# Layer 1's q and k made with the tokens stationary and 512 weight columns moving, turned through DRAM, in a two-layer graph attention kernel

## The chip, the core and the metric

The kernel runs on one core of one Trainium2 chip. The core has five engines with instruction queues of their own, each worked off in order: TensorE (PE) multiplies matrices, VectorE (DVE) and ScalarE (ACT) work element by element and may read PSUM, where PE leaves its results, GpSimd (POOL) works element by element on SBUF, and SyncE (SP) issues the transfers (DMAs) between DRAM and SBUF. They wait for each other by semaphores. The metric is the device time of one execution in microseconds (us), as the median of several runs.

## What is computed

Two layers of masked attention, each followed by a residual sum and a normalisation over the 512 features. x is 128 graphs of 128 nodes and 512 features, adj a mask of 128 by 128 for each graph; all numbers are 32-bit floats.

```python
# layer 0: 4 heads of 64
q, k, v = x @ Wq, x @ Wk, x @ Wv
sim = where(adj, q @ k.T * 64**-0.5, -max)
x = layernorm(x + softmax(sim) @ v @ Wo + bo)
# layer 1: 8 heads of 64
h = layernorm(x) * gamma + beta
q, k, v = split(h @ w_qkv.T)
s = where(adj | eye, q @ k.T * 64**-0.5, -1e9)
x = layernorm(x + softmax(s) @ v @ w_out.T + b_out)
```

## The kernel before

Graphs are handled in groups of two (G = 2, so 256 tokens and 64 groups). Every group goes through a pipeline of steps; step(s) (line 736) is the body for s = 2 to 63, opening (line 698) is what stands before it, closing (line 825) runs twice and last (line 879) once. A step works on several groups at once: layer 0's projections (product_0) of group s, layer 0's scores and softmax of group s-1, its attention and output projection (out_product(0, ...)) of group s-2, layer 1's q and k (qk) of group s-2, layer 1's scores, softmax and v of group s-3, its attention and output projection (out_product(1, ...)) of group s-4.

All projections are written as seven half-size products instead of eight (Strassen's scheme in Winograd's form): sums of halves of the left operand are made on POOL (halves_sums, line 286), those of the weights once at the start. The seven products, numbered 1 to 7 and issued in the order 1, 2, 6, 5, 7, 3, 4, share three PSUM banks: "a", "f" and one of four turning "mm" tiles ("c", INTO in line 297). A product that adds to a bank must wait until the reader of the bank's earlier state is done. ACT copies the banks after products 1, 5 and 6, DVE adds after 2, 3 and 7, ACT copies after 4 (taken, line 333; for layer 0 in lines 392 to 399). Layer 1's q and k come out of PE with features on the partitions: 128 weight columns are stationary and 128 tokens move, eight matmuls a product, each of them two passes on PE (32-bit floats). For v the 128 tokens are stationary and 256 weight columns move.

A transpose of activations or probabilities goes through DRAM: DVE turns 32 by 32 blocks (turn in line 214, blocks in line 523), put (line 201) writes the tile to DRAM, and fetch (line 207) brings it back in four transfers of 32 partitions each, blocks now in place. arrive (line 223) does this for the rows of either layer into the one tile "raw"; probs_arrive for the probabilities. in_order (line 240) and finish (line 249) are ACT's copies out of raw: into xT of layer 0, and with gamma and beta into xT of layer 1. For the first and the last two groups finish_direct (line 264) transposes on PE instead.

The order in which the functions are called is written out by hand, and each engine gets its instructions in that order; nothing is reordered. All transfers are issued by SP, in order: a transfer whose source or target isn't ready holds up those behind it. So where a call stands in step matters on every engine that it uses. Tiles with one tag and one buffer (pool one) are shared by their users in turn. The residual rows of a group stay in R (a ring of six buffers, line 78); load brings the next group's rows and mask, stats (line 601) makes mean and variance on DVE and then, by roots, the reciprocal root on POOL, norms (line 639) normalises on ACT, deferred to the next flush, addend (line 589) scales (layer 1, ACT) and adds the bias (POOL).

Of the kernel before, what the change touches and what calls it, by code (L numbers as in the profile page):

```python
# [17 lines left out]
P = 128  # L18
D = 64
G = 2  # L20
# [7 lines left out]
def kernel(ctx: ExitStack, tc: tile.TileContext, x, adj, wq, wk, wv, wo, bo,  # L28
# [13 lines left out]
    six = ctx.enter_context(tc.tile_pool(name="six", bufs=6))  # L42
    dram = ctx.enter_context(tc.tile_pool(name="dram", bufs=2, space=bass.MemoryType.DRAM))
# [26 lines left out]
    for i in range(4):  # L70
        spare_rows(six, "r", 2)
    for tag, n in (("qk1", 4), ("v1", 2), ("xT1", 2)):
        spare_rows(one, tag, n)

    def load(g):
        if g >= NG:
            return
        R[g] = six.tile([P, G, E], F32, tag="r", name=f"r_{g}")
        M[g] = six.tile([P, G, N], U8, tag="m", name=f"m_{g}")
        nc.sync.dma_start(R[g], x[g * G:(g + 1) * G].rearrange("b n e -> n b e"))  # L80
        nc.sync.dma_start(M[g], adj[g * G:(g + 1) * G].rearrange("b i j -> i b j"))

    R[0] = six.tile([P, G, E], F32, tag="r", name="r_0")
# [30 lines left out]
    gb_raw = const.tile([2 * KC, P], F32, name="gb_raw")  # L114
# [3 lines left out]
    def load_transposed(dst, src, name, scaled=0):  # L118
# [7 lines left out]
        def part(r):  # L126
# [6 lines left out]
            if r * P < scaled:  # L133
                nc.scalar.activation(to, pt, AF.Copy, scale=SCALE)
            elif r % 2:
                nc.scalar.copy(to, pt)
            else:
                nc.vector.tensor_copy(to, pt)
# [17 lines left out]
    w1qk = w1[:, :, :2 * I1].rearrange("p c (t h f) -> p c t h f", t=2, h=2)  # L156
    w1v = w1[:, :, 2 * I1:].rearrange("p c (h f) -> p c h f", h=2)
    wsqk = const.tile([P, 3, KH, 2, I1 // 2], F32, name="wsqk")
    wsv = const.tile([P, 3, KH, I1 // 2], F32, name="wsv")

    def weight_sums(w, ws, *blocks_):

        for c in blocks_:
            if w is w1qk:
                b11, b12 = w[:, c, :, 0], w[:, c, :, 1]
                b21, b22 = w[:, KH + c, :, 0], w[:, KH + c, :, 1]
            else:
                b11, b12 = w[:, c, 0], w[:, c, 1]
                b21, b22 = w[:, KH + c, 0], w[:, KH + c, 1]
# [20 lines left out]
    load_transposed(w1, w_qkv, "w_qkv", scaled=INNER[1])  # L190
# [6 lines left out]
    RATIO, XT, QK, V, QKV = {}, {}, {}, {}, {}  # L197
# [102 lines left out]
    def product(kind, g, i):  # L300
# [6 lines left out]
        w, ws = (w1qk, wsqk) if kind == "qk" else (w1v, wsv)  # L307

        def right(c):
            return {1: lambda: w[:, c, :, 0] if kind == "qk" else w[:, c, 0],  # L310
                    2: lambda: w[:, KH + c, :, 0] if kind == "qk" else w[:, KH + c, 0],
                    3: lambda: w[:, KH + c, :, 1] if kind == "qk" else w[:, KH + c, 1],
                    4: lambda: ws[:, 2, c], 5: lambda: w[:, c, :, 1] if kind == "qk" else w[:, c, 1],
# [8 lines left out]
        if kind == "qk":  # L322
            todo = [(acc[:, (t * 2 + j) * P:(t * 2 + j + 1) * P], right(c)[:, t, j * P:(j + 1) * P],
                     left[:, c], c) for t in range(2) for j in range(2) for c in range(KH)]
        else:
            todo = [(acc[:, :I1 // 2], left[:, c], right(c), c) for c in range(KH)]
        for n, (o, lhsT, rhs, c) in enumerate(todo):

            nc.tensor.matmul(o, lhsT, rhs, start=first and n == 0, stop=n == len(todo) - 1,  # L329
                             skip_group_check=True)  # L330
        taken(kind, g, i, acc)

    def taken(kind, g, i, acc):

        if i == 1:
            if kind == "qk":
                QK[1, g] = one.tile([P, 2 * I1 // P, T], F32, tag="qk1", name=f"qk1_{g}")
            else:
                V[1, g] = one.tile([P, G, I1], F32, tag="v1", name=f"v1_{g}")
        n = 512 if kind == "qk" else I1 // 2  # L340
        src = acc[:, :n]

        def whole(b, h):
            if kind == "qk":

                return QK[1, g].rearrange("p (t h j) n -> p t h j n", t=2, h=2)[:, :, h, :, b * N:(b + 1) * N]
            return V[1, g][:, b, h * n:(h + 1) * n]

        def like(ap, b, h):
            return ap.rearrange("p (t j n) -> p t j n", t=2, j=2) if kind == "qk" else ap  # L350

        if i in (1, 5, 6):
            e = one.tile([P, 512], F32, tag=f"e{i}", name=f"e{kind}{i}_{g}")[:, :n]
            EV[kind, i] = e
            nc.scalar.copy(e, src)  # L355
        elif i == 4:
            nc.scalar.copy(whole(1, 0), like(src, 1, 0))
        elif i in (2, 3, 7):
            b, h, e = {2: (0, 0, 1), 3: (0, 1, 6), 7: (1, 1, 5)}[i]
            nc.vector.tensor_add(whole(b, h), like(src, b, h), like(EV[kind, e], b, h))  # L360

    def product_0(g, *which):
# [5 lines left out]
        for i in which:  # L368
# [5 lines left out]
            if i == 1:  # L374

                QKV[g] = two.tile([P, G, 2, 3, P], F32, tag="qkv0", name=f"qkv0_{g}")
# [4 lines left out]
            acc = ACC[0, bank]  # L381
            todo = [(t, c) for t in range(3) for c in range(KH)]
            for n, (t, c) in enumerate(todo):
                lhsT, rhs = (right[:, c, t], left[:, c]) if t < 2 else (left[:, c], right[:, c, t])
                nc.tensor.matmul(acc[:, t * P:(t + 1) * P], lhsT, rhs, start=first and n == 0,  # L385
# [3 lines left out]
            def whole(b, h):  # L389
                return QKV[g][:, b, h].rearrange("p t n -> p (t n)")  # L390
# [44 lines left out]
    def group_of(s, part):  # L435
        g = s - (3 if part else 1)
# [517 lines left out]
```

## Time and profile before

| what | value |
|---|---|
| median of 3 runs | 2784.76 us (2784.01 to 2785.39) |
| the profiled execution: span from first to last instruction | 2782.9 us (the execution's own time; the median stands 1.9 us above it) |
| PE, DVE, ACT, POOL busy | 99%, 64%, 54%, 63% |
| a step, from first score matmul to the next step's | 42.84 us |
| DMA | 405 MB, mean 146 GB/s, packets take 49.5% of 16 engines' span in the kernel's queue |
| a transfer of 512 KB to DRAM, a fetch of 128 KB: issue to landing | 3.0 to 4.4 us, 3.6 to 4.1 us (medians) |

The page gives busy time of each engine, the chain of work that ended last, and groups of like instructions with their mean duration. A timeline line has start (us), duration (us), engine, line of the kernel, operation, output and inputs, shapes and count; in brackets stands the idle time before it and what ended it. Matmuls overlap on PE, so what a product costs is read from one start to the next, not from the durations. In a table by stretches, each line has the stretch, the busy time of each engine with its count of instructions, the granted clock of PE, and last the DMA share and the rate in GB/s.

### The profile page before, as it was taken

The page shows a single profiled execution, that of the slowest core. Times are in us where ns is not written, and L with a number is a line of the kernel's source. Part 1 is how long each engine was busy: PE and PEld are TensorE (multiplying, and loading weights), DVE is VectorE, ACT ScalarE, POOL GpSimd, SP SyncE. Part 2 cuts the span into 40 slices and gives each one's busy share as a digit, 9 for nine tenths or more (in the row PEclk, how much of TensorE's full clock was granted, in tenths as well). Part 3 has the DMA queues.
Part 4 walks back from the last instruction along what each step waited for, and adds up shares of the span by engine and source line. Part 5 has one row for each costly group of instructions (what it writes and reads, how often), then busy time and mean ns, then how long its engine had stood idle before and what let it go on. Part 6 is the DMA issues. An engine that isn't in the chain of part 4 may idle for free.

```text
span 2782.9 us, 63227 instructions
## 1 busy us (share of the span) xinstructions
PE 2768.0 (99%) x23317; PEld 2609.2 (94%) x23317; DVE 1789.9 (64%) x3303; ACT 1502.5 (54%) x4811; POOL 1752.2 (63%) x2311
## 2 busy tenths in 40 slices
PE   9999999999999999999999999999999999999998
PEld 8999999999999999999999999999999999999997
DVE  5766666666666666666666666666666666666665
ACT  3554555645555556455555564555555645555554
POOL 5656566666565666666656666666566666665664
PEclk9999999999999999999999999999999999999999
DMA  5345455464564554644545546455454464554532
GB/s 170 115 138 173 128 158 154 130 175 138 138 171 127 161 153 129 177 138 138 169 129 161 153 127 177 139 138 166 128 165 148 128 179 136 145 165 126 160 107 69
DMA packets 281812, 405.24 MB, mean 146 GB/s; under 512 B 44696, under 2 KB 206496, under 8 KB 281504
## 3 DMA queue, kind: packets, MB, share of 16 engines
q1 hardware_dynamic: 281504, 401.20, 49.5%
q8 instruction: 185, 3.03, 0.5%
q14 instruction: 123, 1.01, 0.1%
HBM read 205.00 MB, written 196.08 MB: 144 GB/s over the span
## 4 chain that ended last, share of the span: by engine, by line
PE 96%; issue 1%; POOL 1%; DVE 1%; DMA 1%; ACT 0%; SPq 0%; POOLq 0%; ACTq 0%; DVEq 0%
PE qka L329 16%; PE a L385 12%; PE oa L423 12%; PE qkf L329 8%; PE va L329 8%; PE av L575 6%; PE f L385 6%; PE of L423 6%; PE qkc L329 4%; PE vf L329 4%; PE c L385 3%; PE oc L423 3%; PE sc L456 2%; PE sc L462 2%; PE vc L329 2%; PE sc_a L462 2%
## 5 line engine op out<-in xcount | busy, mean ns | idle before, releaser
L514 POOL TENSOR_TENSOR sm<-sm,rec 128x1024 f32<-128x1024 f32 x192 | 364.1, 1896 | 383.4 <-DVE rec L513 383.1
L505 ACT ACTIVATE sm<-sm,nmax 128x128 f32<-128x128 f32 x1536 | 595.2, 393 | 4.9 <-DVE nmax L496 4.3
L596 POOL TENSOR_TENSOR r<-r,bias 128x1024 f32<-128x1024 f32 x128 | 302.0, 2359 | 63.5 <-ACT r L595 63.5
L427 DVE TENSOR_TENSOR r<-oa,r 128x256 f32<-128x256 f32 x508 | 212.3, 418 | 199.7 <-PE oa L423 191.6
L292 POOL TENSOR_TENSOR xs<-xT 128x256 f32<-128x256 f32 x256 | 189.4, 740 | 211.0 <-ACT xT L246 164.9
L505 ACT ACTIVATION_READ_ACCUMULATOR sm<-sm,nmax 128x1 f32 x1536 | 294.8, 192 | 0.0
L355 ACT COPY eqk<-qka 128x512 f32<-128x512 f32 x128 | 75.0, 586 | 349.3 <-PE qka L329 349.3
L490 DVE COPY_PREDICATED sm<-m,sc 128x512 f32<-128x512 uint8 x256 | 173.0, 729 | 134.9 <-PE sc L456 134.9
L329 PE MATMUL qka<-xs,wsqk 128*128 128x128 f32 x2048 | 249.7, 275 | 0.3 <-POOL xs L292 0.3
L329 PE MATMUL qkf<-xs,w 128*128 128x128 f32 x2048 | 249.8, 275 | 0.0
L529 DVE STREAM_TRANSPOSE turnedp<-sm 128x1024 f32<-128x1024 f32 x189 | 234.0, 1238 | 17.1 <-DMA scrp<-turnedp 11.8
L329 PEld LDWEIGHTS qka<-xs,wsqk 128*128 128x128 f32 x2048 | 239.0, 192 | 0.5 <-POOL xs L292 0.5
L329 PEld LDWEIGHTS qkf<-xs,w 128*128 128x128 f32 x2048 | 239.0, 192 | 0.0
L360 DVE TENSOR_TENSOR qk<-qka,eqk 128x512 f32<-128x512 f32 x64 | 44.3, 692 | 291.1 <-PE qka L329 286.1
L496 DVE TENSOR_REDUCE nmax<-sm 128x8 f32<-128x1024 f32 x192 | 226.4, 1206 | 0.1
L423 PE MATMUL oa<-wso,so 128*128 128x256 f32 x760 | 206.0, 380 | 0.7 <-DVE r L427 0.7
L423 PE MATMUL of<-wo,so 128*128 128x256 f32 x760 | 205.6, 379 | 0.7 <-POOL so L292 0.7
L615 POOL TENSOR_SCALAR ve<-mv 128x2 f32<-128x2 f32 x191 | 40.8, 214 | 261.3 <-DVE mv L608 255.1
L641 ACT ACTIVATE r<-r,shift,root 128x512 f32<-128x512 f32 x254 | 192.4, 807 | 8.7 <-POOL shift L630 4.7
L476 POOL MEMSET sm<- 128x1024 f32 x192 | 178.8, 951 | 0.0
L607 DVE BATCH_NORM_STATS2 st<-r 128x6 f32<-128x512 f32 x254 | 171.7, 676 | 4.4
L423 PEld LDWEIGHTS of<-wo,so 128*128 128x128 f32 x760 | 144.1, 190 | 20.9 <-POOL so L292 1.1
(159 smaller groups left out, 6799.9 us busy)
## 6 DMA issues: line engine op xcount, KB each, us to landing
scrp<-turnedp SPq DMA_DIRECT2D x189, 512.0 KB, 3.0
pT<-scrp SPq DMA_DIRECT2D x756, 128.0 KB, 4.1
scr<-turned SPq DMA_DIRECT2D x121, 512.0 KB, 4.4
raw<-scr SPq DMA_DIRECT2D x484, 128.0 KB, 3.6
r<-in_x_dram SPq DMA_DIRECT2D x63, 512.0 KB, 3.9
out_dram<-r SPq DMA_DIRECT2D x63, 512.0 KB, 5.0
m<-in_adj_dram SPq DMA_DIRECT2D x64, 32.0 KB, 3.7
raw_r<-in_L_gnn_w_qkv_dram SPq DMA_DIRECT2D x8, 256.0 KB, 4.2
```

What stands on the lines that cost most here:

```text
L292: nc.gpsimd.tensor_tensor(o, a0, a1, op=op)
L329: nc.tensor.matmul(o, lhsT, rhs, start=first and n == 0, stop=n == len(todo) - 1, skip_group_check=True)
L385: nc.tensor.matmul(acc[:, t * P:(t + 1) * P], lhsT, rhs, start=first and n == 0, stop=n == len(todo) - 1, skip_group_check=True)
L423: nc.tensor.matmul(acc, left[:, c], right[:, c], start=first and c == 0, stop=c == hk - 1, skip_group_check=True)
L427: nc.vector.tensor_add(part, acc, part)
L476: nc.gpsimd.memset(sm, NEG1 if part else NEG0)
L496: nc.vector.tensor_reduce(NMAX[part], SM[part], AX.X, ALU.max, negate=True)
L505: nc.scalar.activation(sm[:, i, k, :], sm[:, i, k, :], AF.Exp, bias=nmax[:, i, k:k + 1], accum_out=total[:, i, k:k + 1])
L514: nc.gpsimd.tensor_tensor(SM[part], SM[part], rec[:, :, :, None].to_broadcast([P, 2, K1, N]), op=ALU.mult)
L529: nc.vector.transpose(t.rearrange("p q (h r) -> p q h r", r=32), SM.pop(part).rearrange("p i k (q r) -> p q (i k) r", r=32))
L596: nc.gpsimd.tensor_tensor(R[g], R[g], (bias0, bias1)[l][:, None, :].to_broadcast([P, G, E]), op=ALU.add)
L641: nc.scalar.activation(R[g][:, b], R[g][:, b], AF.Identity, bias=shift[:, b:b + 1], scale=root[:, b:b + 1])
```

## The change

Layer 1's q and k are now made as v is: 128 tokens are stationary and 512 weight columns move, so a product has two matmuls in place of eight. The half split of the weight columns is now k (first) and q (second). The results have tokens on the partitions, so they are turned: DVE transposes 32 by 32 blocks after products 2, 7, 3 and 4 (taken_tokens), SP puts k of each graph and q of both to DRAM, q_arrive and k_arrive fetch them, and ACT copies q in order with the scale (q_in_order); k is used from the fetched tile as it lies. The scale 64**-0.5 is no longer in the weights. The last two groups (PLAIN_QK) keep the old form. Layer 1 works on a group one step later: qk on s-3 with v on s-3, scores on s-4, attention and output on s-5; there are three closing steps, and layer 1's rows always go through DRAM. Calls in step stand in a new order: norms of layer 1, load and both halves of finish now stand among layer 0's products, qk stands where v stood, and v with layer 1's output projection stands at the end of the step, with layer 1's stats and addend behind them.

To make room, layer 0's q, k and v have one buffer (qkv0) in which v alternates between two places, several tiles share tags (so and aT of layer 0 with the two tiles of q, the turned q with raw, the turned k with xT0), R gets a seventh buffer and layer 1's v a second one. closing has the same changes of order as step; it isn't shown.

```diff
+    seven = ctx.enter_context(tc.tile_pool(name="seven", bufs=7))
     dram = ctx.enter_context(tc.tile_pool(name="dram", bufs=2, space=bass.MemoryType.DRAM))
     ps_mm = ctx.enter_context(tc.tile_pool(name="ps_mm", bufs=4, space=PSUM))
...
-        spare_rows(six, "r", 2)
-    for tag, n in (("qk1", 4), ("v1", 2), ("xT1", 2)):
-        spare_rows(one, tag, n)
+        spare_rows(seven, "r", 2)
+    for pool, tag, n in ((one, "kt", 2), (two, "v1", 2), (two, "v1", 2), (one, "xT1", 2)):
+        spare_rows(pool, tag, n)
...
@@ -153,20 +152,17 @@
     I1 = INNER[1]
     KH = KC // 2
 
-    w1qk = w1[:, :, :2 * I1].rearrange("p c (t h f) -> p c t h f", t=2, h=2)
+    w1qk = w1[:, :, :2 * I1].rearrange("p c (h f) -> p c h f", h=2)
...
@@ -319,45 +315,111 @@
         elif first:
             ACC[kind, which] = ps_st.tile([P, 512], F32, tag=which, name=f"{kind}{which}_{g}")
         acc = ACC[kind, which]
-        if kind == "qk":
-            todo = [(acc[:, (t * 2 + j) * P:(t * 2 + j + 1) * P], right(c)[:, t, j * P:(j + 1) * P],
-                     left[:, c], c) for t in range(2) for j in range(2) for c in range(KH)]
+        n = I1 if kind == "qk" else I1 // 2
+        if kind == "qk" and g in PLAIN_QK:
+            todo = [(acc[:, j * P:(j + 1) * P], right(c)[:, j * P:(j + 1) * P], left[:, c])
+                    for j in range(K1) for c in range(KH)]
         else:
-            todo = [(acc[:, :I1 // 2], left[:, c], right(c), c) for c in range(KH)]
-        for n, (o, lhsT, rhs, c) in enumerate(todo):
-
-            nc.tensor.matmul(o, lhsT, rhs, start=first and n == 0, stop=n == len(todo) - 1,
+            todo = [(acc[:, :n], left[:, c], right(c)) for c in range(KH)]
+        for m, (o, lhsT, rhs) in enumerate(todo):
+            nc.tensor.matmul(o, lhsT, rhs, start=first and m == 0, stop=m == len(todo) - 1,
                              skip_group_check=True)
-        taken(kind, g, i, acc)
-
-    def taken(kind, g, i, acc):
+        (taken_v if kind == "v" else taken_features if g in PLAIN_QK else taken_tokens)(g, i, acc[:, :n])
+
+    PLAIN_QK = (NG - 2, NG - 1)
+
+    def tap(kind, g, i, src, scale=1.0):
+        EV[kind, i] = one.tile([P, 512], F32, tag=f"e{i}", name=f"e{kind}{i}_{g}")[:, :src.shape[1]]
+        if scale == 1.0:
+            nc.scalar.copy(EV[kind, i], src)
+        else:
+            nc.scalar.activation(EV[kind, i], src, AF.Copy, scale=scale)
+
+    def taken_v(g, i, src):
 
         if i == 1:
-            if kind == "qk":
-                QK[1, g] = one.tile([P, 2 * I1 // P, T], F32, tag="qk1", name=f"qk1_{g}")
-            else:
...
+        if i == 4:
+            nc.scalar.copy(to, src)
+        else:
+            nc.vector.tensor_add(to, src, EV["v", e])
+
+    QO, KT, TQ, SCRQ = {}, {}, {}, {}
+
+    def taken_tokens(g, i, src):
+
+        if i in (1, 5, 6):
+            return tap("qk", g, i, src)
+        if i == 4:
+            done = src
+        else:
+            done = EV["qk", {2: 1, 3: 6, 7: 5}[i]]
+            nc.vector.tensor_add(done, src, done)
+        what, b = {2: ("k", 0), 7: ("q", 1), 3: ("q", 0), 4: ("k", 1)}[i]
+        if i in (2, 7):
+            TQ[what] = one.tile([P, 4, G, K1 * 32], F32, tag={"k": "xT0", "q": "raw"}[what],
+                                name=f"t{what}_{g}")
+            SCRQ[what] = dram.tile([P, 4, G, K1 * 32], F32, tag=f"scr{what}", name=f"scr{what}_{g}")
+        t = TQ[what][:, :, b]
+        nc.vector.transpose(t.rearrange("p q (c j) -> p q c j", j=32),
+                            done.rearrange("p (c q j) -> p q c j", q=4, j=32))
+        if what == "k":
+            nc.sync.dma_start(SCRQ[what][:, :, b], t)
+        elif i == 3:
+            nc.sync.dma_start(SCRQ[what], TQ[what])
+
+    def k_tile(g):
+        KT[g] = one.tile([P, 4, G, K1, 32], F32, tag="kt", name=f"kt_{g}")
+        return KT[g]
+
+    def q_tile(g, b):
+        QO[g, b] = one.tile([P, K1, N], F32, tag=f"qo{b}", name=f"qo{b}_{g}")
+        return QO[g, b]
+
+    def q_arrive(g):
+
+        if 0 <= g < NG and g not in PLAIN_QK:
+            RAW["q"] = one.tile([P, 4, G, K1, 32], F32, tag="raw", name=f"rawq_{g}")
+            fetch(RAW["q"].rearrange("p a b c j -> p a (b c j)"), SCRQ["q"].rearrange("p q b x -> p q (b x)"))
+
+    def k_arrive(g):
+
+        if 0 <= g < NG and g not in PLAIN_QK:
+            fetch(k_tile(g).rearrange("p a b c j -> p a (b c j)"), SCRQ["k"].rearrange("p q b x -> p q (b x)"))
+
+    def q_in_order(g):
+
+        if 0 <= g < NG and g not in PLAIN_QK:
+            for b in range(G):
+                nc.scalar.activation(q_tile(g, b).rearrange("p c (a j) -> p a c j", a=4), RAW["q"][:, :, b],
+                                     AF.Copy, scale=SCALE)
+
...
+    def taken_features(g, i, src):
+
+        if i in (1, 5, 6):
...
-            nc.scalar.copy(whole(1, 0), like(src, 1, 0))
-        elif i in (2, 3, 7):
-            b, h, e = {2: (0, 0, 1), 3: (0, 1, 6), 7: (1, 1, 5)}[i]
-            nc.vector.tensor_add(whole(b, h), like(src, b, h), like(EV[kind, e], b, h))
+            nc.scalar.copy(plain_keys(g, 1), src)
+        else:
+            b, e = {3: (0, 6), 7: (1, 5)}[i]
+            nc.vector.scalar_tensor_tensor(q_tile(g, b).rearrange("p c n -> p (c n)"), src, SCALE,
+                                           EV["qk", e], op0=ALU.mult, op1=ALU.add)
 
     def product_0(g, *which):
+            odd = g % 2
             todo = [(t, c) for t in range(3) for c in range(KH)]
             for n, (t, c) in enumerate(todo):
                 lhsT, rhs = (right[:, c, t], left[:, c]) if t < 2 else (left[:, c], right[:, c, t])
-                nc.tensor.matmul(acc[:, t * P:(t + 1) * P], lhsT, rhs, start=first and n == 0,
+                at = (t + odd) % 3
+                nc.tensor.matmul(acc[:, at * P:(at + 1) * P], lhsT, rhs, start=first and n == 0,
                                  stop=n == len(todo) - 1, skip_group_check=True)
             src = acc[:, :3 * P]
 
             def whole(b, h):
-                return QKV[g][:, b, h].rearrange("p t n -> p (t n)")
+                return qkv0[:, b, h, 1 - odd:4 - odd].rearrange("p t n -> p (t n)")
...
     def group_of(s, part):
-        g = s - (3 if part else 1)
+        g = s - (4 if part else 1)
...
-                        q_, k_ = (QKV[g][r, b, h // 2, i, :] for i in range(2))
+                        q_, k_ = (qkv0[r, b, h // 2, i, :] for i in (1, 2))
                         nc.tensor.matmul(ps[h % 2][:, b * K0 + h // 2, :], q_, k_, start=True, stop=True)
             else:
-                t = slice((part - 1) * N, part * N)
+                b = part - 1
                 for h in range(HEADS[1]):
                     r = slice((h % 2) * D, (h % 2 + 1) * D)
-                    q_, k_ = (QK[1, g][r, i * K1 + h // 2, t] for i in range(2))
-                    nc.tensor.matmul(ps[h % 2][:, h // 2, :], q_, k_, start=True, stop=True)
+                    nc.tensor.matmul(ps[h % 2][:, h // 2, :].rearrange("p (a j) -> p a j", j=32),
+                                     QO[g, b][r, h // 2], keys_of(g, b, h // 2, r), start=True, stop=True)
...
-            g = s - (2, 4)[l]
+            g = s - (2, 5)[l]
             if not 0 <= g < NG:
                 continue
             K = (K0, K1)[l]
             if part != 2:
-                AT[l, g] = one.tile([P, G, K, N], F32, tag=f"aT{l}", name=f"aT{l}_{g}")
+                AT[l, g] = one.tile([P, G, K, N], F32, tag=("qo1", "aT1")[l], name=f"aT{l}_{g}")
...
-        so = SO[l, g] = one.tile([P, 4, K // 2, N], F32, tag=("so", "xs0")[l], name=f"so{l}_{g}")
+        so = SO[l, g] = one.tile([P, 4, K // 2, N], F32, tag=("qo0", "xs0")[l], name=f"so{l}_{g}")
...
     def step(s):
 
-        direct = s in (2, 3)
         made = scores(s)
-        load(s + 1)
         if s > 2:
             in_order(s)
             sums(0, s)
+        arrive(1, s - 3)
         masked(made, s, 0, 1, 2)
         attend(s)
-        maxima(s, 0)
-        if s > 3:
-            maxima(s, 1)
+        maxima(s, 0, 1)
         out_sums(0, s - 2)
         exps(s, 0, 0)
         product_0(s, 1)
         exps(s, 0, 1)
         out_product(0, s - 2, 1, 2, 5)
-        if s == 3:
-            maxima(s, 1)
         maxima(s, 2)
         product_0(s, 2)
+        flush()
+        load(s + 1)
         normalised(s, 0)
         out_product(0, s - 2, 6, 3)
         exps(s, 1, 0)
         stats(0, s - 2, 0)
         product_0(s, 6)
         exps(s, 1, 1)
+        finish(s - 3, 0)
         out_product(0, s - 2, 7)
         product_0(s, 5)
         out_product(0, s - 2, 4)
         stats(0, s - 2, 1)
         exps(s, 2, 0)
         product_0(s, 7)
-        exps(s, 2, 1)
+        finish(s - 3, 1)
         normalised(s, 1)
         product_0(s, 3)
         blocks(s, 0)
-        flush()
+        exps(s, 2, 1)
         product_0(s, 4)
-        if direct:
+        if s in (2, 3):
             prepare(len(setup) - (s == 2))
-        else:
-            turn(1, s - 2)
-        out_sums(1, s - 4)
-        v(s - 3, 1, 2)
-        out_product(1, s - 4, 1)
-        if not direct:
-            arrive(1, s - 2)
         blocks(s, 1)
-        probs_arrive(s, 0)
-        v(s - 3, 6, 5)
-        out_product(1, s - 4, 2)
-        normalised(s, 2)
-        v(s - 3, 7, 3)
-        turn(0, s + 1)
-        v(s - 3, 4)
-        flush(latest)
-        cleared(s + 1, 0, 1)
-        if direct:
-            finish_direct(s - 2)
-        else:
-            finish(s - 2, 0)
+        qk(s - 3, 1)
         if s == 2:
             weight_sums(w1qk, wsqk, 1)
             prepare(1)
-        out_product(1, s - 4, 6, 5)
-        if not direct:
-            finish(s - 2, 1)
-        out_product(1, s - 4, 7, 3, 4)
+        flush()
+        qk(s - 3, 2)
+        normalised(s, 2)
+        probs_arrive(s, 0)
+        qk(s - 3, 6, 5)
+        flush(latest)
+        turn(1, s - 2)
+        probs_arrive(s, 1)
+        qk(s - 3, 7)
+        cleared(s + 1, 0, 1)
+        out_sums(1, s - 5)
         blocks(s, 2)
-        probs_arrive(s, 1)
-        stats(1, s - 4, 0)
-        stats(1, s - 4, 1)
+        qk(s - 3, 3, 4)
+        out_product(1, s - 5, 1, 2)
+        q_arrive(s - 3)
+        v(s - 3, 1, 2)
+        out_product(1, s - 5, 6)
+        turn(0, s + 1)
+        k_arrive(s - 3)
+        probs_arrive(s, 2)
+        v(s - 3, 6, 5)
+        out_product(1, s - 5, 5)
+        v(s - 3, 7, 3)
+        q_in_order(s - 3)
+        out_product(1, s - 5, 7)
+        v(s - 3, 4)
         arrive(0, s + 1)
-        probs_arrive(s, 2)
         cleared(s + 1, 2)
+        out_product(1, s - 5, 3, 4)
         addend(0, s - 1)
+        stats(1, s - 5, 0)
+        stats(1, s - 5, 1)
+        addend(1, s - 4)
         with_self(s - 2)
-        qk(s - 2, 1, 2, 6)
-        flush()
-        qk(s - 2, 5)
-        addend(1, s - 3)
-        qk(s - 2, 7, 3, 4)
...
+    for s in range(NG, NG + 3):
+        closing(s)
```

## The prediction

> **What bounds the kernel now.** I read the head of the page first, then the chain that ended last, then one step of the timeline, then SP's waits and the DMA issues.
>
> ```profile
> span 2782.9 us, 63227 instructions
> PE 2768.0 (99%) x23317; PEld 2609.2 (94%) x23317; DVE 1789.9 (64%) x3303; ACT 1502.5 (54%) x4811; POOL 1752.2 (63%) x2311
> ...
> PE 96%; issue 1%; POOL 1%; DVE 1%; DMA 1%; ACT 0%; SPq 0%; POOLq 0%; ACTq 0%; DVEq 0%
> ```
>
> TensorE (PE) is busy 99% of the span and is 96% of the last chain; the waits of PE name nine causes, 8.0 us in all. So any step in which another engine makes PE wait is lost time at once. The span stands 1.9 us under the median of the runs (2784.76); I work in differences and put them on the median. The timeline of one step:
>
> ```profile
> 1435.24 1.16 PE L456 MATMUL sc<-qkv 64*128 64x128 f32 x16
> 1437.05 0.73 POOL L292 TENSOR_TENSOR xs<-xT 128x256 f32<-128x256 f32 x1 [2.66 <-ACT xT L246]
> ...
> 1440.05 0.46 POOL L292 TENSOR_TENSOR so<-aT 128x128 f32<-128x128 f32 x1
> ...
> 1440.89 1.16 PE L385 MATMUL a<-xT,w 128*128 128x128 f32 x8
> ...
> 1443.20 0.59 PE L423 MATMUL of<-wo,so 128*128 128x256 f32 x2
> ...
> 1453.40 1.03 PE L329 MATMUL va<-w,xT 128*128 128x256 f32 x4
> 1454.26 1.03 PE L329 MATMUL vc<-w,xT 128*128 128x256 f32 x4
> ...
> 1465.49 1.95 PE L329 MATMUL qka<-xT,w 128*128 128x128 f32 x16
> ...
> 1467.27 1.95 PE L329 MATMUL qkc<-xT,w 128*128 128x128 f32 x16
> ...
> 1468.94 0.27 POOL L615 TENSOR_SCALAR ve<-mv 128x2 f32<-128x2 f32 x1 [1.31 <-DVE mv L608]
> ...
> 1470.52 0.95 POOL L476 MEMSET sm<- 128x1024 f32 x1
> 1471.44 2.37 POOL L596 TENSOR_TENSOR r<-r,bias 128x1024 f32<-128x1024 f32 x1
> ...
> 1478.08 1.16 PE L456 MATMUL sc<-qkv 64*128 64x128 f32 x16
> ```
>
> First column start, second duration. A step takes 42.84 us (1435.24 to 1478.08), start to start. A qk product (16 PE passes of 128 columns) takes 1.785 from start to start, 111.6 ns a pass; a v product (4 passes of 256) takes 0.863, 215.8 ns a pass. GpSimd (POOL) starts the four sums of xT (3.0 us) only 1.8 us into the step, then the sums of aT; the first of these is ready at 5.35, and the product that needs it (of<-wo,so) starts at 7.96. These 2.6 us are the slack I shall spend. SP and the DMAs:
>
> ```profile
> SPq L210 <- DMA scr<-turned: 162.2, 61, 4.4
> ```
>
> ```profile
> scrp<-turnedp SPq DMA_DIRECT2D x189, 512.0 KB, 3.0
> pT<-scrp SPq DMA_DIRECT2D x756, 128.0 KB, 4.1
> scr<-turned SPq DMA_DIRECT2D x121, 512.0 KB, 4.4
> raw<-scr SPq DMA_DIRECT2D x484, 128.0 KB, 3.6
> ```
>
> ```profile
> 1473.00:1475.00 2.00, 2.00 (x21) 2.00 (x20) 0.31 (x1) 1.80 (x4) 0.93 (x2) 1.00 1.15 215
> ```
>
> A fetch waits on SP for its put to land, 2.7 us a time, and all that SP issues later stands behind. The last line is a 2 us stretch late in the step: its last two numbers are the DMA share, 1.15, and 215 GB/s: the DMA engines are full there already.
>
> **The change part by part.** E is the moment at which a step's first score matmul starts.
>
> *Products.* Seven qk products a group become 4 passes of 512 columns each, for 62 groups (the last two keep the old form). No row has 512. The straight line through 111.6 and 215.8 gives 424 ns, so 1.70 a product; twice the 256-column pass gives 1.726. I take 1.712: 0.073 saved, 0.51 a step (0.41 to 0.62), 32 us in 62 groups. The Trainium skill ("TensorE: Matmul & The Clock Gate", Back-to-back issue gap) gives sustained figures of 81 ns at 128 columns and 131 ns at 512, by which the qk passes would shrink to 0.40 of today's 12.5 us, a saving of 7.5 a step; the step from 111.6 to 215.8 here denies such a discount.
>
> *ACT.* One copy of 0.59 goes, two in-order copies of q (about 0.6 each, row xT<-raw) come. Moved ahead of the evictions of layer 0: the norms of layer 1 (1.41) and the two halves of finish (1.04 each). From the first exp to the end of the copy of product_0(5), in the new order: 16 exps of 0.385 (6.2), two copies (0.7), norms (1.4), half of finish (1.0) and the copy itself (0.4): 9.7 us, where today it is 7.2. product_0(3) writes the same bank and waits for it; below.
>
> *DVE.* Four transposes of 128x512 a group, 0.67 each (row L219's), 2.7 us a step on an engine busy 64%. They cost PE nothing where DVE runs ahead; the next user of bank "a" (v's product 1) comes 1.73 us of PE after qk(4), and the last transpose ends about 1.2 after it: 0.5 of cover, and past this each us is a us. The statistics of layer 1 (two of 0.79) and with_self (0.35) now stand after the step's last product, so masking starts at E+2.6, not E+1.25.
>
> *POOL, the first chain.* Today layer 1's statistics precede qk and 12 us of PE cover what hangs on them. Now out_product(1,...,4) is the last product. From E: DVE add 0.25+0.4, statistics 1.6, so roots may start at E+2.3; roots 1.6 (1468.94 to 1470.52), addend(1) 2.37, sums(0) 3.0, first out_sum 0.54, semaphore 0.1: E+9.9. The product that needs it is due at E+7.97 (row above). PE waits 1.9 us in every step. This is already more than the 0.51 saved.
>
> *SP and DMA, the second chain.* Three puts and eight fetches come to a step, 2 MB on 6.3 MB. The one tile raw holds layer 1's rows, then q turned, q fetched, and only then the next group's rows, in a row. Let T be the end of qk(4), 12.1 us (14 products of 0.863) before E. q's transpose is done at T+0.55 (DVE is late by blocks(1), whose POOL product stands behind sums(1)); its put lands 4.4 later by the row, or up to 6 later, since two fetch sets of 512 KB (2.3 us each at 224 GB/s) and two puts (1.3 each) are issued in the 4.7 us ahead of it; I take T+6.5. Behind it on SP: q's fetch 1.76, a put 0.4, k's fetch 1.76, pT's 2.0, then the next rows' fetch, last issue 1.3 later, landing 3.6: T+17.4, E+5.3; 6.1 with the queue still full, 3.7 if the put takes the row's 4.4. ACT in_order takes 1.2, then sums(0), out_sum: E+8.6 to E+11.05 for the same product. So PE's wait is 1.9 to 3.1; I take 2.9, near the upper end, since the stretch was full before the change. ACT's first exp comes at E+8.7 then (in_order, three copies), product_0(3) may start at E+18.5 and is due at 15.5+2.9: no more is lost there. k's fetch lands about E+1.9 with its scores due at E+1.0; that wait lies inside the 2.9. [...]
>
> *Bought with nothing.* The load of x after a wait for out (4.6 us on SP, moved to about E+14 to E+19): the next put is due at E+21; without that cover up to 4 us. One buffer for layer 0's q, k, v: read before E+4, written after E+8. Seventh R buffer, weight layout: no added work.
>
> *Ends.* Four groups of direct transposes go: 32 of 0.11, 3.6 us. Step 2 has no qk, so step 3 meets its probabilities and rows early: 13 us of waits; steps 4 and 5 have the q round trip with only 6 us of v as cover: about 14. A third closing step has 22.3 us of PE and a softmax chain of near 28; with the two before it about 19. In all 46, between 20 and 60.
>
> *Sum.* 2784.8 - 32 - 3.6 + 58 steps x 2.9 (168) + 46 = 2963.
>
> **The rivals.** *Both chains hidden.* POOL reaches the sums in time, or ACT and DMA run ahead. For it: POOL is busy only 63%, and no engine but PE is full. Against: the first chain has no DMA in it and every link has a row. It decides where PE's wait falls below 0.5 a step: then 2784.8 - 35.6 + 20 = 2769, on the other side (2750 to 2795).
>
> *Only the first chain.* Rows arrive in time: 58 x 1.9, ends 35: 2894. This lies in my forecast's own range.
>
> *DMA full for good.* 2 MB more at 215 GB/s are 9.7 us in a tail of 20: if the rows come at E+8, the wait is 5 and the time 3085. Against: DMA is busy under half of the span.
>
> *512 columns don't stream.* If a pass takes 446 ns or more the 32 us are gone; 512-column rows are missing, so this can't be excluded, and it lifts every case by 32.
>
> **How the numbers follow.** Slower by the chains (2865 to 3035): 0.78. Both hidden: 0.15, of which 0.12 faster, 0.02 same, 0.01 slower. DMA full: 0.07. A difference under 0.2% (5.6 us) can't be told from none. The range leaves out the hidden case and the worst: 2860 to 3035. Chances: faster 0.12, same 0.02, slower 0.86.
>
> **What would show it.** Steps 45.2 apart; PE's share near 93%; PE waiting for POOL's so and for ACT's xT at the head of each step (about 1 to 3 us a step together), for kt at the scores; SP waiting for the put of q; the qk pass near 429 ns. A step of 42.4 with no such waits would make me wrong, and a step of 44.2 would say that only POOL's chain binds.

## The result, and the profile after

The changed kernel takes 3121.77 us (median of 4 runs, 3109.18 to 3122.88), the kernel before 2784.43: a ratio of 1.12, 95% interval 1.1181 to 1.122. The forecast was slower, 2963 us with a range of 2860 to 3035. The direction holds, the size doesn't: the loss is 337 us where 178 were forecast.

The profiled execution spans 3107.4 us. It was the fastest of the four (3109.18 us): the median lies 12.6 us above it, and what sets the executions 14 us apart isn't known. Head of the page, busy time and the last chain:

```profile
span 3107.4 us, 54173 instructions
PE 2864.2 (92%) x18077; PEld 2233.8 (72%) x18077; DVE 1944.9 (63%) x3545; ACT 1525.3 (49%) x4871; POOL 1744.5 (56%) x2311
...
PE 51%; DMA 20%; ACT 7%; POOL 7%; DVE 6%; SPq 6%; issue 4%; ACTq 0%; DVEq 0%; POOLq 0%
```

PE fell from 96% to 51% of the chain that ended last, and DMA came in with 20%. No compute engine has a higher share than before (only the packets of the DMA queue do, 58.4% for 49.5%): this is a kernel of waits. Where the 324.5 us between the spans (3107.4 - 2782.9) lie is read from the first score matmul of each step: 6.2 up to step 6, 281.7 in the 58 steps 6 to 63 (4.86 each: 47.71 for 42.85), 36.6 from step 64 to the end. One step on PE, from the timeline:

```profile
1393.38 1.16 PE L517 MATMUL sc<-qkv 64*128 64x128 f32 x16
1396.38 0.46 PE L522 MATMUL sc_a<-kt,qo 64*128 64x128 f32 x2 [1.83 <-DMA kt<-scrk]
1397.56 0.34 PE L522 MATMUL sc_f<-kt,qo 64*128 64x128 f32 x1 [0.72 <-DMA kt<-scrk]
...
1398.53 2.06 PE L522 MATMUL sc<-kt,qo 64*128 64x128 f32 x15
...
1403.88 1.16 PE L446 MATMUL a<-xT,w 128*128 128x128 f32 x8
...
1406.22 0.70 PE L484 MATMUL of<-wo,so 128*128 128x256 f32 x2
...
1417.08 1.88 PE L325 MATMUL qka<-w,xT 128*128 128x512 f32 x4
1418.80 1.88 PE L325 MATMUL qkc<-w,xT 128*128 128x512 f32 x4
...
1441.28 0.94 PE L517 MATMUL sc<-qkv 64*128 64x128 f32 x12
```

With E = 1393.38, PE waits for k's fetch at the scores of layer 1, then the second graph's scores and the attention go slowly, and the product that needs the sums of aT (of<-wo,so) starts at E+12.84, where it was E+7.96. So 4.88 us are gone by then. The same head of the step on POOL and ACT:

```profile
1395.61 0.27 POOL L676 TENSOR_SCALAR ve<-mv 128x2 f32<-128x2 f32 x1 [7.60 <-DVE mv L669]
...
1397.22 2.36 POOL L657 TENSOR_TENSOR r<-r,bias 128x1024 f32<-128x1024 f32 x1
...
1401.51 1.14 ACT L243 COPY xT<-raw 128x512 f32<-128x512 f32 x2 [6.60 <-DMA raw<-scr]
...
1402.72 0.73 POOL L289 TENSOR_TENSOR xs<-xT 128x256 f32<-128x256 f32 x1 [3.15 <-ACT xT L243]
...
1405.71 0.46 POOL L289 TENSOR_TENSOR so<-aT 128x128 f32<-128x128 f32 x1
```

Roots start at E+2.2 and addend ends at E+6.2, but then POOL stands idle for 3.15 us: the rows of the group land only at E+8.1. In this step the first sum of aT ends just when PE has come to the product, so it looks as if the late rows and the late k held PE to the same moment. They do so only in some steps. Three steps later PE is at the product early and waits:

```profile
1536.74 1.16 PE L517 MATMUL sc<-qkv 64*128 64x128 f32 x16
...
1546.33 1.16 PE L446 MATMUL a<-xT,w 128*128 128x128 f32 x8 [1.26 <-ACT xT L243]
...
1550.36 0.70 PE L484 MATMUL of<-wo,so 128*128 128x256 f32 x2 [1.56 <-POOL so L289]
```

Over steps 6 to 63 the product starts 0.51 us behind the start of the first sum of aT in 56 of 58 steps, so it is the rows that hold PE; k comes last only in the other two. Late in the step shown first, DVE finishes q's second transpose and SP goes on:

```profile
1427.64 2.69 SPq L207 DMA_DIRECT2D pT<-scrp  x4
...
1429.11 0.71 DVE L368 STREAM_TRANSPOSE tq<-eqk 128x512 f32<-128x512 f32 x1
...
1430.43 0.45 SPq L201 DMA_DIRECT2D scrp<-turnedp  x1
1430.98 0.38 SPq L373 DMA_DIRECT2D scrq<-tq  x1
1431.45 0.85 SPq L371 DMA_DIRECT2D scrk<-tk  x1
1436.21 2.87 SPq L207 DMA_DIRECT2D rawq<-scrq  x4
1439.18 0.38 SPq L201 DMA_DIRECT2D scr<-turned  x1
1439.66 2.21 SPq L207 DMA_DIRECT2D kt<-scrk  x4
1441.97 1.80 SPq L207 DMA_DIRECT2D pT<-scrp  x4
1443.88 1.81 SPq L207 DMA_DIRECT2D raw<-scr  x4
```

SP puts q and the second half of k, stands for 3.9 us until q has landed, and then issues q's fetch, k's and the rows' one behind the other. That q's four fetches take 2.87 us to issue is not typical: the median over the steps is 1.75.

### The profile page after: what moved, and what is told of

It reads as the page before. It is cut to its first block, busy times and chain, and to the rows that moved or that the text cites. A ratio compares the mean times of both kernels' runs of the same rounds, so it can differ in the third digit from the quotient of the medians.

```text
span 3107.4 us, 54173 instructions
## 1 busy us (share of the span) xinstructions
PE 2864.2 (92%) x18077; PEld 2233.8 (72%) x18077; DVE 1944.9 (63%) x3545; ACT 1525.3 (49%) x4871; POOL 1744.5 (56%) x2311
## 3 DMA queue, kind: packets, MB, share of 16 engines
q1 hardware_dynamic: 430208, 535.46, 58.4%
## 4 chain that ended last, share of the span: by engine, by line
PE 51%; DMA 20%; ACT 7%; POOL 7%; DVE 6%; SPq 6%; issue 4%; ACTq 0%; DVEq 0%; POOLq 0%
PE qka L325 11%; DMA kt<-scrk 7%; PE a L446 7%; DMA raw<-scr 6%; SPq L207 5%; POOL xs L289 5%; PE qkf L325 5%; PE f L446 5%; DMA scrq<-tq 5%; PE oa L484 4%; ACT sm L566 3%; PE qkc L325 3%; PE va L325 3%; PE of L484 3%; PE c L446 2%
## 5 line engine op out<-in xcount | busy, mean ns | idle before, releaser
L334 ACT COPY ev<-va 128x256 f32<-128x256 f32 x128 | 47.6, 372 | 581.2 <-PE va L325 581.2
L243 ACT COPY xT<-raw 128x512 f32<-128x512 f32 x122 | 69.4, 616 | 364.3 <-DMA raw<-scr 299.3
L488 DVE TENSOR_TENSOR r<-of,r 128x256 f32<-128x256 f32 x254 | 107.7, 424 | 206.5 <-PE of L484 199.4
L325 PE MATMUL qkf<-w,xs 128*128 128x512 f32 x496 | 233.1, 592 | 0.0
L325 PE MATMUL qka<-wsqk,xs 128*128 128x512 f32 x496 | 233.1, 592 | 0.0
L398 ACT ACTIVATE qo<-rawq 128x512 f32<-128x512 f32 x124 | 71.2, 621 | 321.8 <-DMA rawq<-scrq 321.8
L325 PEld LDWEIGHTS qkf<-w,xs 128*128 128x128 f32 x496 | 94.3, 190 | 118.6 <-issue 118.3
L325 PEld LDWEIGHTS qka<-wsqk,xs 128*128 128x128 f32 x496 | 94.3, 190 | 118.1 <-issue 103.5
```

Of the source, the lines that this page charges most:

```text
L325: nc.tensor.matmul(o, lhsT, rhs, start=first and m == 0, stop=m == len(todo) - 1, skip_group_check=True)
L488: nc.vector.tensor_add(part, acc, part)
```

## The experiments

e1 to e6, e8 and e9 are one execution each, beside the kernel before on the same chip; e7 and e10 are timed in rounds. Step times are means from step 5 on. Executions of the changed kernel lie 14 us apart, 0.2 us a step, so smaller differences between single executions say little.

**e1_plain and e2_noturn: the order of calls, and the form.** e1 needs one line:

```diff
-    PLAIN_QK = (NG - 2, NG - 1)
+    PLAIN_QK = tuple(range(NG))
```

> The changed kernel with every group in the old form of q and k (128 weight columns stationary, straight into feature order), so no transposes, puts, fetches or in-order copies of q and k; the new order of calls and the turn's delay stay. My theory: the step of 47.7 us is set by the loop q's put, q's fetch, k's fetch, scores (and beside it the next rows behind q in the one tile raw). With the loop gone POOL's chain is left, 1.9 us a step: step 44.7, about 2915 us (2880 to 2940). Rival, the order of calls itself (POOL and ACT behind the step's last product) makes the loss: still 3050 or more. Rival, the 512-column passes make the loss: step 42.8, about 2800.

e2 keeps the 512-column products and their additions and cuts what follows:

```diff
         if i == 4:
-            done = src
+            nc.vector.tensor_copy(FIX["e"], src)
         else:
             done = EV["qk", {2: 1, 3: 6, 7: 5}[i]]
             nc.vector.tensor_add(done, src, done)
-        what, b = {2: ("k", 0), 7: ("q", 1), 3: ("q", 0), 4: ("k", 1)}[i]
...
-                    nc.tensor.matmul(..., QO[g, b][r, h // 2], keys_of(g, b, h // 2, r), ...)
+                    nc.tensor.matmul(..., FIX["k"]..., FIX["k"][r, :, b, h // 2], ...)
```

> The changed kernel with the 512-column products of q and k and their additions, but without their transposes, puts, fetches and in-order copies: the scores of layer 1 read one constant tile instead, so the output is not the reference's. It differs from e1_plain by the form of the products and little else. My theory: 7 products of 1.717 for 7 of 1.785, so 0.48 us a step under e1_plain, about 2885 (POOL's chain stays). Rival, 512 columns cost more than their passes show: no faster than e1_plain.

Measured: 2935.88 and 2907.25 us, steps of 44.92 and 44.44. PE's longest wait in e1, then in e2:

```profile
PE of L484 <- POOL so L289: 97.4, 62, 3.1
```

```profile
PE of L461 <- POOL so L289: 98.3, 62, 3.1
```

Once in each of the 62 steps, 1.6 us, PE waits for the sums of aT: the new order of calls, with the turn's delay and the tiles that go with it, costs 2.07 us a step. The form gives 0.48 a step, 28.6 us in all, as forecast. e1 lies 21 us over my figure, more than half of it since the step is 44.92 and not 44.7 (58 x 0.22 are 13), the rest at the ends.

**e3_stale: the wait apart from the traffic.**

```diff
-                TQ[what] = one.tile(..., tag={"k": "xT0", "q": "raw"}[what], ...)
+                TQ[what] = one.tile(..., tag={"k": "xT0", "q": "pT2"}[what], ...)
+            OLD[what] = SCRQ.get(what)
...
-            fetch(RAW["q"]..., SCRQ["q"]...)
+            fetch(RAW["q"]..., (OLD["q"] or SCRQ["q"])...)
```

(the same for k)

> The changed kernel with the turned q in the tile of part 2's probabilities, and q and k fetched from the scratch of the group before, so that the fetches don't wait for this group's puts: all transfers, bytes and places in SP's order stay, and only the wait for the landing goes. The scores use the q and k of the group before, so the output is not the reference's. My theory, the wait on SP sets the loop: the fetches of q, k and the next rows go out about 5 us sooner, POOL's chain is left, step 44.3 to 45, 2890 to 2930. Rival, the DMA engines are simply full in the tail: the fetches land as late as before, 3050 or more.

Measured: 2990.18 us, steps of 45.81. Neither theory's number. Against e2 the transposes, transfers and in-order copies cost 1.37 us a step without a wait for this group's puts; against the changed kernel the wait costs 1.97. So the step is 42.85 + 2.07 (order) - 0.48 (form) + 1.37 (added work and traffic) + 1.97 (wait) = 47.78, the mean from step 5 on. These are differences of one run to the next, so they must add up; in another order of removal the parts could be others. I had the wait as the whole of it. Without it q's fetch goes out 4.0 us earlier, but the rows land only 1.9 earlier, since q's four fetches then take 3.4 us to issue and not 1.9 (means of steps 6 to 62). And in e3 too the product starts 0.51 us behind the first sum's start, in all of steps 6 to 63: what is left of the loss still comes by way of the rows.

**e4_addend and e5_plain_early: the chain on POOL.**

```diff
         maxima(s, 0, 1)
         out_sums(0, s - 2)
+        addend(1, s - 5)
         exps(s, 0, 0)
...
         stats(1, s - 5, 1)
-        addend(1, s - 4)
```

> The changed kernel with addend of layer 1 (ACT 1.34, POOL 2.37 us) moved from the end of the step to the next step, behind layer 0's output sums: POOL comes to the sums of xT at E+3.9 instead of E+6.2. My theory, the rows of the next group come only at E+8 and hold the sums anyway: no gain, 3090 to 3160, rather slower since ACT's part now stands before the exps. Rival, POOL's chain adds up with the rest: 2.0 us or more a step less, 2990 or under.

Measured: 3184.63 us, steps of 49.03, more than the 3160 I allowed. POOL now has time before the rows come, and it is worth nothing; ACT's 1.34 us stand before the exps, and PE waits 62.4 us in all for the eviction of product_0(5), where it was 2.5. e5 puts the same edit on e1 and clears ACT too:

```diff
         product_0(s, 2)
-        flush()
-        load(s + 1)
...
         exps(s, 1, 1)
-        finish(s - 3, 0)
         out_product(0, s - 2, 7)
         product_0(s, 5)
+        flush()
+        load(s + 1)
+        finish(s - 3, 0)
```

> e1_plain with the two chains at the head of the step shortened: addend of layer 1 moved behind layer 0's output sums of the next step (POOL comes to the sums of xT 2.4 us sooner), and on ACT the norms of layer 1 and half of finish moved behind the copy of product_0(5) (2.45 us sooner). My theory: the 2.06 us that e1_plain's step is longer than before's are POOL's chain, with ACT's close behind: both shortened, the step is about 43.5 and the time 2850 (2820 to 2870). Rival: the wait sits elsewhere (masking by DVE 1.35 us later, or the sums waiting for the rows): step 44.5 or more, 2910 or more.

Measured: 2855.07 us, steps of 43.53. With the loop gone, POOL's chain and ACT's behind it are 1.4 of the 2.07 us. The two were moved together, so their shares stay open.

**e6_warm: the slow clock.** The stretches of the changed kernel behind the wait for k in the step shown first (the third number from the end is the granted clock):

```profile
1398.00:1400.00 2.00, 2.00 (x27) 2.00 (x24) 1.34 (x2) 0.00 (x0) 1.58 (x1) 0.59 1.00 195
1400.00:1402.00 2.00, 2.00 (x21) 1.78 (x20) 1.67 (x3) 0.49 (x1) 0.00 (x0) 0.56 0.03 9
```

```diff
+            if part == 1 and g not in PLAIN_QK:
+                for i in range(14):
+                    nc.tensor.matmul(ps[i % 2][:, :N], wo0[:, 0, :P], wo0[:, 0, :N], start=True, stop=True)
```

> The changed kernel with 14 idle matmuls (28 passes of 128 columns, 3.1 us) on PE between the scores of layer 0 and of layer 1, where PE waits about 2.9 us for k. Their results are overwritten. The changed kernel's granted clock is 0.56 to 0.59 for about 3 us behind that wait; PE is kept busy here. My theory: the clock stays at 1.00, but the product that waits for the sums of aT still stands at E+12.8 since the next rows hold it: no more than 30 us gained, 3085 to 3125. Rival, the clock loss is a cost of its own: 1.6 us a step less, 3030.

Measured: 3122.28 us, steps of 47.91, the clock 1.00 in the same place. From the arrival of k to layer 0's product 1 PE needs 6.3 us in the step shown and 4.8 in e6, but it then waits for the sums of aT instead. The wait for them, in the changed kernel and then in e6:

```profile
PE of L484 <- POOL so L289: 56.9, 50, 1.6
```

```profile
PE of L484 <- POOL so L289: 76.4, 60, 1.6
```

The trace of the changed kernel says the same without e6. Its clock is reduced in 29 of steps 6 to 63 and not in the other 29 (51 us of PE's time in all, 0.9 a step). Where it is reduced, PE waits 0.4 us for the sums on average, and the steps are 47.9 apart; where it isn't, 1.6, and they are 47.5 apart. So the slow clock used up time that PE would have waited.

**e8_rows_out and e9_rows_out_warm: which of the two arrivals holds.**

```diff
-            TQ[what] = one.tile(..., tag={"k": "xT0", "q": "raw"}[what], ...)
+            TQ[what] = one.tile(..., tag={"k": "xT0", "q": "pT2"}[what], ...)
...
-            RAW["q"] = one.tile(..., tag="raw", ...)
+            RAW["q"] = one.tile(..., tag="xT0", ...)
...
         qk(s - 3, 2)
+        turn(0, s + 1)
...
         probs_arrive(s, 1)
+        arrive(0, s + 1)
```

> The changed kernel with the next group's rows taken out of the loop of q: the turned q lies in the tile of part 2's probabilities, the fetched q in that of xT0, so raw is free behind finish; the rows are turned behind qk's second product and fetched behind part 1's probabilities, ahead of q's put on SP. My theory: the wait for k's fetch and the slow clock behind it (2.9 and 1.6 us) hold PE as well as the rows did, and k's fetch now goes out up to 2 us later: no gain, steps of 47 to 49.5, 3080 to 3230. Rival, the rows behind q were the one bound: 2 us a step less, 3000 or under.

> e8_rows_out with the 14 idle matmuls of e6_warm while PE waits for k. With the rows out of the way the clock is the next thing: my theory says 1.2 to 1.8 us a step under e8_rows_out (70 to 105 us), where e6_warm gained nothing. Rival, the slow clock costs nothing here either: within 25 us of e8_rows_out.

Measured: 3291.20 and 3209.54 us, steps of 50.77 and 49.38. The rows do come early (ACT copies them at E+5.2 on average, not E+8.2), and yet nothing is gained: four more fetches stand before q's put on SP, q's fetch waits for k's second put, whose tile it now takes, and goes out 3.0 us later, and PE waits for q at the scores:

```profile
PE sc_a L522 <- ACT qo L398: 118.2, 42, 4.2
```

That is worse than I expected of it (3230 at most). But with the rows early the clock counts: it is reduced in 50 of steps 6 to 63, the idle matmuls gain 82 us here and nothing in e6. As e8 made q and k later too, it doesn't show what the rows alone are worth. An estimate from the trace of the changed kernel: before the product PE waits for the rows or the sums 0.4 us in the steps with a reduced clock and 2.2 in the others (0.69 + 1.56), so with k as it is, rows in time could give about 1.3 us a step.

**e7_half_turn and e10_half_turn_end: the same form, a turn away from its use.** The order of calls goes back to that of the kernel before; q and k have a whole step for their way:

```diff
-    PLAIN_QK = (NG - 2, NG - 1)
+    PLAIN_QK = ()
...
-            TQ[what] = one.tile(..., tag={"k": "xT0", "q": "raw"}[what], ...)
+            TQ[what] = one.tile(..., tag="turned", bufs=2, ...)
...
     def step(s):
...
         made = scores(s)
+        load(s + 1)
         if s > 2:
             in_order(s)
             sums(0, s)
-        arrive(1, s - 3)
+        q_arrive(s - 3)
+        k_arrive(s - 3)
...
+        v(s - 3, 1, 2)
+        q_in_order(s - 3)
...
+        qk(s - 2, 7, 3, 4)
```

(against the changed kernel; the other calls that go back to their old places, and closing, are left out)

> All groups in the form with 512 weight columns and turned through DRAM, layer 1 a turn later, but in the order of calls of the kernel before: q and k at the end of the step, fetched in the first half of the next (where the DMA engines stood still before), copied in order behind v's second product, used by the scores of the step after. The turned q and k take turns in the ring of two tiles of the other transposes. My theory: the loss comes from what stands behind the step's last product and from the loop through DRAM within 12 us of PE, not from the form: here both have a whole step, PE waits for nothing, step 42.35, 62 x 0.51 gained, a third closing step lost: 2767 (2755 to 2782). Rival, the added DMA and DVE work costs wherever it stands (1.3 us a step, e3_stale over e2_noturn): 2840 or more.

Measured: 2780.14 us (10 runs, 2777.07 to 2782.77), ratio to before 0.9982, interval 0.9973 to 0.9992. Head of its page, and its longest wait of PE:

```profile
PE 2744.8 (99%) x17941; PEld 2142.7 (77%) x17941; DVE 1975.5 (71%) x3561; ACT 1538.2 (55%) x4873; POOL 1754.1 (63%) x2311
```

```profile
PE av L637 <- DMA pT<-scrp: 10.6, 2, 7.0
```

The step is 42.35 us, the number forecast, with all of the added DVE and DMA work in it. One step of the kernel before, then one of e7 (the last two numbers are the DMA share and GB/s):

```profile
1435.24:1478.08 42.84, 42.84 (x363) 40.47 (x362) 27.68 (x51) 23.39 (x75) 27.28 (x36) 1.00 0.52 149
```

```profile
1378.42:1420.77 42.35, 42.35 (x279) 33.13 (x278) 30.51 (x55) 23.45 (x76) 26.74 (x36) 1.00 0.71 202
```

So neither the form nor the traffic costs by itself, but where they stand. Of 29.3 us gained by step 64, 25.2 are lost again at the end, where the third closing step has too little for PE and the probabilities come late. e10 shortens that:

```diff
+        if s == NG + 2:
+            normalised(s, 2)
+            blocks_direct(s, 1)
+            blocks_direct(s, 2)
...
     def last():
...
+        v(s - 4, 1, 2, 6)
         attend(s)
```

> e7_half_turn with a shorter end: in the third closing step the probabilities of layer 1 are transposed on PE instead of through DRAM, and in the last step three of v's products stand ahead of the attention. In e7_half_turn PE waits 7.0 and 3.6 us there for the probabilities, and runs at a clock of 0.85. My theory: the step stays 42.35 and 8 to 12 us of the end are gained: 2770 (2766 to 2774). Rival, the softmax chain of the last two groups holds the end anyway: 2777 to 2780.

Measured: 2778.04 us (8 runs, 2776.44 to 2780.19), ratio 0.9975, interval 0.9965 to 0.9986: 0.25% faster than the kernel before. About 2 us came of the 8 to 12, and the runs of e7 and e10 overlap; PE now waits for the normalisation in place of the transfer, as the rival said:

```profile
PE pt L609 <- POOL sm L576: 4.7, 2, 4.1
```

## Why the prediction was right in direction and wrong in size

*Products.* Right. A product takes 1.717 (1417.08 to 1418.80) where 1.712 was taken, 429 ns a pass.

*POOL, the first chain.* Right where it binds: e1's product starts at E+9.7 (forecast E+9.9), and the order of calls costs 2.07 us a step (forecast 1.9). In the changed kernel the chain is there to the tenth (roots at E+2.2, addend's end at E+6.2) but something later covers it.

*SP and DMA, the second chain.* Here the working failed, at "I take T+6.5", in the issue times behind it and in the landing of the rows, that is, in the term T+17.4 for the next rows. Times from T on, T being the end of qk(4) (1429.10 in the step shown; E comes 12.2 later):

| | forecast | step shown | mean of steps 6 to 62 |
|---|---|---|---|
| q's put landed, q's fetch goes out | 6.5 | 7.1 | 7.2 |
| k's fetch goes out | 8.7 | 10.6 | 9.7 |
| probabilities' fetch goes out | 10.4 | 12.9 | 12.2 |
| rows' fetch goes out | 12.4 | 14.8 | 14.1 |
| rows landed | 17.4 | 20.6 | 20.1 |

The put landed 0.7 late: in the step shown q's second transpose ended at T+0.7 (forecast T+0.55), but SP issued the put only at T+1.9, as four fetches of probabilities took 2.7 us to issue, not 2.0, and a put stood between. The issue of what stands behind cost 1.0 more than forecast, k's fetch the most (2.4 on average for 1.76). From the first issue of the rows' fetch to the landing it took 6.0, where 4.9 were put. So the rows came at E+8 and not at E+5.3, and k not at E+1.9 but, in the step shown, between E+3.0 and E+4.2. PE's wait of "1.9 to 3.1; I take 2.9" was 5.4 (4.86 + 0.51), and 58 times the difference of 2.5 is 143 of the 159 us missing; 12.6 more are the distance of the profiled execution from the median. The mechanism was right (put, wait on SP, rows, sums, product), its links were too short by 2.7 us together. Two slips of the working change little: its own terms add up to T+17.3, and the first sum of aT is ready at 5.27 by the rows shown (1440.05 + 0.46), not at 5.35.

*The clock.* No term of the forecast. It was reduced in half of the steps, 1.6 us of PE's time in the step shown and 0.9 on average, but e6 shows that this alone didn't make the time longer.

*ACT.* "No more is lost there" was nearly right: PE waits 0.29 us there in the step shown and 2.5 us, eight times, in the whole run. e4 shows how little room was left.

*Ends.* 46 forecast, less 3.6 for the transposes; 42.8 measured. That the two agree is partly luck: steps 3 to 5 lost 19.9 us where 27 were put, step 2 became 14.0 shorter, and 36.6 were lost behind step 64, where 19 were put.

*The rivals.* "DMA full for good" had the right place and size (rows at E+8, wait 5, 3085 us) and 0.07. Its reason is half right at most: e3 puts 1.37 us a step on the added work and traffic, 1.97 on the wait, and e7 carries the same traffic at no cost. The range stopped at 3035 because I gave the landing times of the rows as bounds, though the change itself adds a third to the transfers beside them.

## What to carry to other kernels

A round trip through DRAM is priced by what the queue looks like with the round trip in it: rows of today's trace were its lower end here, issue times included. Put the use a full turn of the pipeline away from the making, where the DMA engines stand idle (e7), before asking whether the form is worth it. Where two late arrivals stand close to each other at one instruction, shortening the one that doesn't come last shows nothing (e6), and it counts once the other is out of the way (e9). Which of them comes last is read at the instruction itself, in every step: one step shown here looked like a tie, and 56 of 58 were not k's.

## What the runs showed of the hardware

SP was held longer by the issue of the same four fetches of 128 KB, by what stood before them: q's, which follow a wait in the changed kernel, took 1.75 us (median of steps 6 to 63), k's, which follow q's and a put, 2.31; in e3, where q's don't wait, they took 3.41. How this depends on what is in flight wasn't tested.

The granted clock was 1.00 or 0.50 in all records of these traces, and in the changed kernel it changed on a grid of 3.41 us. The window of the grid before the reduced one of the step shown, and that one (PE's busy time stands behind the first comma):

```profile
1394.92:1398.34 3.42, 1.24 (x16) 1.11 (x18) 2.11 (x5) 0.00 (x0) 2.48 (x5) 1.00 1.01 240
1398.34:1401.75 3.41, 3.41 (x34) 3.19 (x32) 2.76 (x5) 0.24 (x1) 1.24 (x1) 0.50 0.49 95
```

PE waited 1.83 and 0.72 us there. In steps 6 to 63 of the changed kernel PE was busy for 13 to 57% of the window before each reduction, and for 54% or more of all windows that were followed by the full clock; so a window about half idle was enough, and whether a wait reduced the clock depended on how it fell on the grid (half of the steps). A wait of 1.56 us in e1 left it at 1.00. The Trainium skill ("TensorE: Matmul & The Clock Gate", Part 1) says that the gate passes half of the pulses after an idle window of about 3.4 us and all again after a busy one; the half and the 3.4 us agree with these records, but the window before need not be idle.
